# A decoder layer's feed-forward gates on one core: the fourth and fifth products in two levels, and a fixed order of the engines

## The chip, the core and the metric

The kernel runs on one core of one Trainium2 chip. A core has a matrix engine (TensorE, PE in the profile; its weight loads are shown apart as PEld), three engines for element-wise work (VectorE or DVE, ScalarE or ACT, GpSimd or POOL) and SyncE (SP), which here only issues transfers. Matmul results go to eight banks of PSUM, each holding 128 x 512 float32 numbers. The metric is the time of one execution on the device, in microseconds (us).

## The reference

Three blocks, each on a layernorm of x and each added to x: a mamba2 layer followed by an MLP, a product of two fake-quantised matrices, and the feed-forward this case is about (B = 2, S = 512, HID = 1024, INTER = 3584):

```python
def _binary_diff_weight(w, base):
    d = w - base
    coeff = jnp.mean(jnp.abs(d))
    return base + coeff * jnp.sign(d)
W1, W2, W3 = (_binary_diff_weight(w, m) for w, m in ((w1, mean_w1), (w2, mean_w2), (w3, mean_w3)))
gate = jnp.einsum('bsh,ih->bsi', hidden_states, W1)
up = jnp.einsum('bsh,ih->bsi', hidden_states, W3)
h = jax.nn.silu(gate) * up
x = x + jnp.einsum('bsi,hi->bsh', h, W2)
```

## The kernel before

**Stages.** The blocks run one after the other. The MLP of the first block and the feed-forward are both done by `gates` (names with `m` for the MLP and `f` for the feed-forward), which makes the inner values h and writes them to DRAM, and by `down`, which reads them back and multiplies by the last weight. The coefficients and the signs of the feed-forward's weights are made in earlier stages; the signs lie in DRAM as bfloat16.

**Groups and first-level products.** `gates` goes through 14 groups (`NG`, numbered 0 to 13) of 256 inner features. In a group gate and up (128 features by 128 features, two halves) times the activations (1024 features by 2 x 512 tokens) are one 2 x 2 block product, done with Strassen and Winograd's seven products instead of eight. With U2 = product 1 + product 6 and U3 = U2 + product 7, the four blocks are C11 = 1 + 2, C12 = U2 + 5 + 3, C22 = U3 + 5 and C21 = U3 + 4. Each pair of blocks gives gate and up of one quarter, and so a part of h after Silu on ScalarE (L1045) and a product into the tile h on VectorE (L1047).

**Second level.** Each of the seven has an inner size of 512. `second_level` divides two of them at a time by the same rule once more, side by side in the two halves of its banks: 1 with 2 (called the *first* second-level product, banks named `fm`, result in O12) and 6 with 7 (the *second*, banks `fn`, result in O67). There are seven steps, written below as bank and product number; each step is eight instructions of 128 x 256 at L875:

```python
on_pe(lambda: mm("a", 1))
on_act(lambda: nc.scalar.copy(p1, ps["a"]))
on_pe(lambda: mm("b", 6))
on_dve(lambda: add(u2, p1, ps["b"]))
on_pe(lambda: mm("c", 5))
on_pe(lambda: mm("d", 4))
on_pe(lambda: mm("b", 7, True))
on_dve(lambda: add(u3, p1, ps["b"]))
on_dve(lambda: add(c22, u3, ps["c"]))
on_pe(lambda: mm("a", 2, True))
```

A last step, c3, adds onto bank c. So the steps are a1 b6 c5 d4 b7 a2 c3; p1, u2, u3, c22 and c11 are its intermediate sums (`True` means that a step adds onto what the bank holds). Products 5, 4 and 3 are *plain*: `one` (L963) makes each as two columns of 128 x 512 in two banks (`f6c0` and the like, shown as `f6c`, `f6d`), 16 instructions in all. Products 1 and 2 of groups 0 and 1 are made ahead of the stage by `first_two`, in a plain way (L355).

**Sums on VectorE.** `left` makes the weight sums of the next group that products 3, 5, 6 and 7 need, among them the second level's own left sums, and `outer_left` those of the first second-level product. One of `left`'s sums per group, the fourth of one weight (s4), is made later in the MLP's gates (`take_fourths`). `down_blocks` makes four sums (L202, tiles `fw`) of the last weight, which are stored for `down`; `hidden_blocks` makes four sums of h (tiles `fh`). There is one tile h, written to DRAM by SyncE's queue (`fhd`), as are the sums of the last weight (`fwd`).

**Weights.** `ffn_weight` loads the signs on SyncE's queue into a bfloat16 place (`fpl`, two of them, used in turn; L1450), scales them by the coefficient on ScalarE (L1455), and adds the base weight with an accumulating transfer on GpSimd's queue (L1456). Gate and up weights are loaded two groups ahead, the last weight one group ahead, all three issued after the h store of the group before.

**Order.** Two mechanisms exist. `on_pe`, `on_act` and `on_dve` tie an instruction behind the one before it of the same engine (`issue_after`), which makes the order written in the program the order of the engine. What isn't tied is placed by a scheduler, which moves ready work ahead. The MLP's gates (argument `side` set) use the fixed order. In the feed-forward's gates before the change (`side` is None) the lists are empty and so nothing is tied but what stands in `with tc.issue_after(turn)`: the scheduler chooses.

**Down.** `down` makes seven second-level products over all groups (in the order 1, 6, 2, 5, 3, 7, 4; the first also does step e of product 7; L1117) from operand tiles in twelve places (`f1a..`, `f1b..`); its argument `places` says which operand has which place, and `space` leaves room ahead of them, which decides what earlier tiles the places lie over, and so when their loads can start.

## Time and profile before

| | |
|---|---|
| runs, us | 2402.31, 2405.24, 2404.7 (median 2404.7) |
| profiled execution, us | 2406.59 |
| its span, us | 2404.8 |
| granted clock of TensorE, mean | 0.992 |
| feed-forward gates, from and to, us | 1499.5 to 2103.0 |
| busy there: PE, DVE, ACT, POOL, us | 603.5, 421.6, 136.0, 34.3 |
| feed-forward down, from and to, us | 2103.0 to 2404.8 |
| busy there: PE, DVE, ACT, us | 296.7, 167.8, 6.5 |

The span is from the first to the last instruction in the profile of one execution; what the profiled execution takes beside it is 1.8 us. Busy time is the time in which an engine had an instruction, so an engine at full share sets the time of a stage, if its work there is needed. A line of the chain or of the order in time begins with the time from the span's start and the duration, then the engine, the bank or tile and the line of the program, and how many instructions it stands for; what ended an idle time stands in brackets with an arrow. Where two tiles stand with `<-`, the first is written and the others are read.

### The profile page before, as it was taken

What the parts mean: (1) busy time and instruction counts of PE and PEld (TensorE: products, weight loads), DVE (VectorE), ACT (ScalarE), POOL (GpSimd) and SP (SyncE); (2) the same over time, 40 slices, a digit from 0 to 9 for tenths busy, and PEclk for the clock granted to TensorE, in tenths of its full rate; (3) what the DMA queues carried; (4) which work ended last, traced back from release to release, by engine and by line L of the source; (5) the groups of instructions that cost most, each with busy time, mean ns of one, the idle gap of its engine ahead of it and who ended that gap; (6) DMA issues with size and microseconds to landing.
All of it is one profiled execution on the core that took longest, in us unless ns stands there. A gap on an engine that the chain in (4) does not pass through costs nothing.

```text
span 2404.8 us, 23488 instructions
## 1 busy us (share of the span) xinstructions
PE 2356.8 (98%) x8740; PEld 1597.7 (66%) x8740; DVE 1648.5 (69%) x2429; ACT 606.8 (25%) x776; POOL 204.2 (8%) x246
## 2 busy tenths in 40 slices
PE   7999999989999999999999999999999999999999
PEld 5445444446676676677888784676676676688888
DVE  5657777567878878865555656686766766665554
ACT  3345460333243243210000425222222222100000
POOL 1124211201011011000000110000000000000000
PEclk8999999999999999999999999999999999999999
DMA  4353541668888888838746472676676676786651
GB/s 159 114 200 120 186 169 70 176 243 319 306 332 341 303 333 340 289 147 310 222 144 183 130 204 68 182 201 202 163 196 201 166 193 197 243 255 194 192 173 63
DMA packets 183633, 494.49 MB, mean 206 GB/s; under 512 B 21472, under 2 KB 125920, under 8 KB 152544
## 3 DMA queue, kind: packets, MB, share of 16 engines
q1 hardware_dynamic: 155360, 334.65, 40.3%
q0 software_dynamic: 23552, 149.96, 21.7%
q10 hardware_dynamic: 4608, 8.39, 0.9%
q8 instruction: 69, 1.13, 0.2%
q14 instruction: 44, 0.36, 0.0%
HBM read 349.26 MB, written 145.75 MB: 206 GB/s over the span
## 4 chain that ended last, share of the span: by engine, by line
PE 73%; DVE 16%; DMA 4%; issue 3%; ACT 2%; SPq 1%; POOL 0%; DVEq 0%; ACTq 0%; POOLq 0%
PE op L769 3%; DVE sw L202 2%; DVE mpl L199 2%; DVE mo L199 1%; DVE down L202 1%; SPq L1106 1%; DVE mpl L202 1%; ACT smean_w L1273 1%; DVE acc L635 1%; PE ma L355 1%; DMA m4b<-mwd 1%; PE dps L503 1%; PE fa L355 1%; PE xa L1375 1%; DVE mh L1047 1%
## 5 line engine op out<-in xcount | busy, mean ns | idle before, releaser
L1273 ACT ACTIVATE smean_w<-sw 128x2048 bf16<-128x2048 f32 x34 | 65.0, 1911 | 173.5 <-DVE sw L202 173.5
L1455 ACT ACTIVATE fw<-fpl,coeff 128x2048 f32<-128x2048 bf16 x38 | 76.1, 2004 | 91.6 <-DMA fpl<-sign 18.7
L1456 POOL DMA_DIRECT2D fw<-in_mean_w x42 | 36.5, 868 | 530.1 <-ACT fw L1455 476.6
L202 DVE TENSOR_TENSOR sw<-sw,smean_w 128x2048 f32<-128x2048 f32 x34 | 77.6, 2282 | 0.0
L1274 ACT ACTIVATE sw<-sw 128x2048 f32<-128x2048 f32 x34 | 64.9, 1910 | 1.1
L414 POOL TENSOR_TENSOR raw<-raw,base 128x1024 f32<-128x1024 f32 x16 | 41.6, 2602 | 203.6 <-DMA base<-in_mean_w 60.9
L769 PE MATMUL op<-wout,mz 128*128 128x512 f32 x128 | 56.6, 592 | 0.0
L1045 ACT ACTIVATE fo<-fo 128x512 f32<-128x512 f32 x42 | 26.2, 625 | 90.8 <-DVE fo L199 90.7
L1275 POOL DMA_DIRECT2D sign<-smean_w x34 | 18.3, 538 | 292.3 <-ACT smean_w L1273 292.2
L769 PEld LDWEIGHTS op<-wout,mz 128*128 128x128 f32 x128 | 23.9, 190 | 27.7 <-issue 27.3
L202 DVE TENSOR_TENSOR down<-down 128x512 f32<-128x512 f32 x56 | 38.1, 681 | 0.1
L1045 ACT ACTIVATE mo<-mo 128x512 f32<-128x512 f32 x28 | 17.7, 632 | 70.8 <-DVE mo L199 70.8
L199 DVE TENSOR_TENSOR fo<-fo 128x1024 f32<-128x1024 f32 x26 | 31.8, 1225 | 1.7
L355 PE MATMUL fa<-x3T,fw 128*128 128x512 f32 x64 | 30.4, 625 | 2.1 <-ACT fo L361 2.1
L199 DVE TENSOR_TENSOR hid<-hid,op 128x512 f32<-128x512 f32 x24 | 15.9, 683 | 24.0 <-PE op L769 24.0
L1045 ACT ACTIVATE mpl<-mpl 128x512 f32<-128x512 f32 x14 | 8.8, 630 | 89.4 <-DVE mpl L199 89.4
L202 DVE TENSOR_TENSOR fh<-fh 128x512 f32<-128x512 f32 x42 | 29.0, 690 | 1.0
L202 DVE TENSOR_TENSOR mh<-mh 128x512 f32<-128x512 f32 x42 | 28.9, 689 | 0.9
L1264 POOL DMA_DIRECT2D smean_w<-in_mean_w x34 | 18.2, 534 | 129.8 <-DMA sign<-smean_w 42.9
L1375 PE MATMUL xa<-c,c1T 128*128 128x512 bf16 x128 | 28.8, 379 | 0.0
L101 POOL TENSOR_TENSOR q_r<-q_e,mhalf 128x1 f32<-128x1 f32 x8 | 7.0, 877 | 235.2 <-DVE q_e L97 222.1
L1047 DVE TENSOR_TENSOR fh<-fo 128x512 f32<-128x512 f32 x42 | 26.6, 680 | 0.2
(2289 smaller groups left out, 5924.9 us busy)
## 6 DMA issues: line engine op xcount, KB each, us to landing
fw<-in_mean_w POOLq DMA_DIRECT2D x42, 1024.0 KB, 13.6
sw<-in_w POOLq DMA_DIRECT2D x34, 1024.0 KB, 7.7
smean_w<-in_mean_w POOLq DMA_DIRECT2D x34, 1024.0 KB, 7.6
mwd<-down SPq DMA_DIRECT2D x14, 1792.0 KB, 5.7
mhd<-mh SPq DMA_DIRECT2D x13, 1792.0 KB, 10.0
fhd<-fh SPq DMA_DIRECT2D x13, 1792.0 KB, 8.1
fpl<-sign SPq DMA_DIRECT2D x38, 512.0 KB, 8.9
sign<-smean_w POOLq DMA_DIRECT2D x34, 512.0 KB, 6.0
```

Of the source, the lines that this page charges most:

```text
L199: return nc.vector.tensor_tensor(out_, x, y, ALU.add)
L202: return nc.vector.tensor_tensor(out_, x, y, ALU.subtract)
L355: nc.tensor.matmul(ps[x], w[:, 4 * p + k, :P], act[0][:, 4 * p + k, :], start=not p and k == 0, stop=k == 3, skip_group_check=p > 0,)
L414: sub_ = nc.gpsimd.tensor_tensor(w, w, self.base[n % 2], ALU.subtract).ins
L769: nc.tensor.matmul(ps, A[p][:, k, t * P : t * P + P], B[p][:, k, :], start=(k == 0), stop=(k == 3))
L1045: on_act(lambda: nc.scalar.activation(o[:, 0], o[:, 0], AF.Silu))
L1047: nc.vector.tensor_tensor(h[:, slot, :], o[:, 0], o[:, 1], ALU.mult)
L1273: on_act(lambda: nc.scalar.activation(sg, w, AF.Sign))
L1274: on_act(lambda: nc.scalar.activation(w, w, AF.Abs, accum_out=sums[:, j, 2 * i : 2 * i + 1]))
L1375: nc.tensor.matmul(ps, self.c1T[:, k, c : c + P], self.c2[k // 4][:, k % 4, hs], start=(k == 0), stop=(k == KC - 1))
L1455: nc.scalar.activation(dst, src, AF.Identity, scale=coeff[:, j : j + 1])
L1456: nc.gpsimd.dma_start(dst, a[base][i].rearrange("p a b -> p (a b)"), accum_op=ALU.add)
```

## The change

Products 5 and 4 become a third second-level product (banks `fr`, result in O12), from group 2 on, put behind product 3, which now comes first of the plain ones. In groups 0 and 1 products 3, 5 and 4 stay plain and are made in this order, in banks that go round, and `onto` adds them to the blocks. The third product's parts: its left operands come from `third_left` (from the left operands of products 5 and 4), its right ones from `third_right`, once, in group 2, both in VectorE's list between u2 and u3 of the second product. With `early` its step a2 stands ahead of d4: a1 b6 c5 a2 d4 b7 c3. The results are added to C12, C22 and C21 in `finished_third`, run in the next group after its first step, together with the Silus; `last_products` makes the products into h and `put` the sums and the store of h.

`third` being set, the feed-forward's gates use the fixed order of TensorE, ScalarE and VectorE, now for all the sums too (`fix`). Banks go round in eight (X for the first, Y for the second product, Z for product 3 and the third). The sums of the last weight stand behind u2 of the third product (`down_sums`). The two weights of the group after next are asked for at the end of a group and the last weight with the late Silus (`next_weights`). One buffer each instead of two for p1, for the last weight and for each of the two s4 tiles; new tiles for the third's sums (`y54`, `ex`); `down` has no space ahead and other places. Products 1 and 2 of groups 0 and 1 stay as they are. Blank lines are left out below:

```diff
-    def down_blocks(b, t):
+    def down_blocks(b, t, fix=lambda fn: fn()):
...
+        fix(lambda: sub(t3, b22, b12))
...
+    POOLS = dict(t8=1, w=2, w1=2, raw=2, ap=1, hp=1, o1=1, o12=2, o67=1, px=2, s23=1, s4=2, y12=1, y67=1, y54=1, ex=1, b4=2, t4=1)
...
-    def second_level_right(b, t2, t3, t4):
+    def second_level_right(b, t2, t3, t4, fix=lambda fn: fn()):
...
+    def second_level_left(g_, u_, s1, s2, s3, s4, fix=lambda fn: fn()):
...
-    def second_level(name, banks, p1, A, B, O, copied=lambda: None, summed=lambda: None):
+    def second_level(name, banks, p1, A, B, O, copied=lambda: None, summed=lambda: None, early=False):
...
-                        ps[x][:, q, :], A[i][:, q, k, :], B[i][:, q, k, :],
+                        ps[x][:, q, :], A[i][:, q, k, :], B[i][q][:, k, :] if isinstance(B[i], tuple) else B[i][:, q, k, :],
...
         on_pe(lambda: mm("c", 5))
+        if early:
+            on_pe(lambda: mm("a", 2, True))
+            on_act(lambda: nc.scalar.copy(c11, ps["a"]))
         on_pe(lambda: mm("d", 4))
         on_pe(lambda: mm("b", 7, True))
         on_dve(lambda: add(u3, p1, ps["b"]))
         on_dve(lambda: add(c22, u3, ps["c"]))
-        on_pe(lambda: mm("a", 2, True))
-        on_act(lambda: nc.scalar.copy(c11, ps["a"]))
+        if not early:
+            on_pe(lambda: mm("a", 2, True))
+            on_act(lambda: nc.scalar.copy(c11, ps["a"]))
...
-    def gates(name, act, acts, g, pl, weights, down_weight, begun, ex, side):
+    def gates(name, act, acts, g, pl, weights, down_weight, begun, ex, side, third=()):
...
+        fix = on_dve if third else lambda fn: fn()
+        act_last[:] = [None]
+        dve_last[:] = [None]
+        pe_last[:] = [None]
...
+            B12 = B54 = A54 = None
             def outer_left(i, gw, uw):
                 gv, uv = (w[:, :, :P].rearrange("p (q k) c -> p q k c", q=2) for w in (gw, uw))
-                y = pl["y12"].tile([P, 1 if side else 4, 2, 2, P], F32, tag="y", name=f"{name}y12_{i}")
-                if side:
-                    return second_level_left(gv, uv, uv[:, :, :2], y[:, 0], *pl["y12_"])
-                return second_level_left(gv, uv, *(y[:, j] for j in range(4)))
+                more = pl.get("y12_", ())
+                y = pl["y12"].tile([P, 3 - len(more), 2, 2, P], F32, tag="y", name=f"{name}y12_{i}")
+                return second_level_left(gv, uv, uv[:, :, :2], *(y[:, j] for j in range(3 - len(more))), *more, fix=fix)
+            def third_left(i, gw, uw):
+                gv, uv = (w[:, :, P:].rearrange("p (q k) c -> p q k c", q=2) for w in (gw, uw))
+                y = pl["y54"].tile([P, 3, 2, 2, P], F32, tag="y", name=f"{name}y54_{i}")
+                return second_level_left(gv, uv, uv[:, :, :2], *(y[:, j] for j in range(3)), fix=on_dve)
+            def third_right():
+                b5, b4 = (
+                    second_level_right(b.unsqueeze(1), *(x[:, q : q + 1] for x in third), fix=on_dve) for q, b in enumerate((B[5], B[4]))
+                )
+                return {j: (b5[j][:, 0], b4[j][:, 0]) for j in b5}
...
-                    four = pl["s4"].tile([P, 4, P], F32, tag=x, bufs=1 if side and x == "g" else 2, name=f"{name}{x}{i}s4")
-                    sub(two[:, 1], a11, a21)
-                    add(a21, a21, a22)
-                    sub(two[:, 0], a21, a11)
+                    four = pl["s4"].tile([P, 4, P], F32, tag=x, bufs=1 if third or x == "g" else 2, name=f"{name}{x}{i}s4")
+                    fix(lambda: sub(two[:, 1], a11, a21))
+                    fix(lambda: add(a21, a21, a22))
+                    fix(lambda: sub(two[:, 0], a21, a11))
                     fourths.append(lambda four=four, a12=a12, two=two: sub(four, a12, two[:, 0]))
-                    if not side or not i or x == "u":
-                        fourths.pop()()
+                    if not i or x == "u":
+                        fix(fourths.pop())
                     s23.append(two)
                     A.append({3: four, 4: a22, 5: a21})
                 y = pl["y67"].tile([P, 3, 2, 2, P], F32, tag="y", name=f"{name}y67_{i}")
-                return A, second_level_left(s23[0], s23[1], s23[1][:, :, :2], *(y[:, j] for j in range(3)))
+                return A, second_level_left(s23[0], s23[1], s23[1][:, :, :2], *(y[:, j] for j in range(3)), fix=fix)
...
+                more = third and i > 1
+                if more:
+                    X, Y, Z = ([(4 + 14 * (i - 2) + o + j) % 8 for j in range(6)] for o in (0, 4, 8))
+                    X, Y = X[:4], Y[:4]
                 def one(x, p, onto=False, into={}):
                     if not onto:
-                        into[x] = [bank(X["ccdd".index(x) + j], f"{name}{i}{x}{j}") for j in range(2)]
+                        into[x] = [bank((Z if more else X)["ccdd".index(x) + j], f"{name}{i}{x}{p}{j}") for j in range(2)]
...
                 if i in begun:
                     O12 = begun[i]
+                    for part in late:
+                        part()
+                    take_fourths()
...
-                    c, d = one("c", 5), one("d", 4)
+                    c, d = (one("c", 3), one("d", 5)) if third else (one("c", 5), one("d", 4))
                 p1 = pl["px"].tile([P, 2, Q], F32, tag="p", name=f"{name}p67_{i}")
                 O67 = pl["o67"].tile([P, 2, 2, L], F32, tag="o", name=f"{name}o67_{i}")
                 def summed67(i=i, O12=O12):
-                    if side:
-                        side(on_dve)
+                    nonlocal A54, B54
+                    side(on_dve)
+                    if i > 1:
+                        on_dve(lambda: add(O12[:, 1], O12[:, 0], O12[:, 1]))
+                    if third:
+                        if i == 2:
+                            B54 = third_right()
                         if i > 1:
-                            on_dve(lambda: add(O12[:, 1], O12[:, 0], O12[:, 1]))
+                            A54 = third_left(i, *coming[0])
+                        on_act(lambda: nc.scalar.activation(O12[:, 1, 0], O12[:, 1, 0], AF.Silu))
                 second_level(f"{name}n{i}", Y, p1, A67, B67, O67, summed=summed67)
                 on_dve(lambda: add(O67[:, 0], O12[:, 0], O67[:, 0]))
                 turn = on_dve(lambda: add(O67[:, 1], O67[:, 0], O67[:, 1]))
-                if i:
-                    c = one("c", 5)
-                for j in range(2):
-                    add(O12[:, 0, j], O67[:, 1, j], c[j])
-                if i:
-                    d = one("d", 4)
-                for j in range(2):
-                    blocks21 = add(O67[:, 1, j], O67[:, 1, j], d[j]).ins
-                one("c", 3, True)
+                h = pl["hp"].tile([P, 7, L], F32, tag="h", name=f"{name}h{i}")
+                if third:
+                    turn = on_dve(lambda: nc.vector.tensor_tensor(h[:, 0, :], O12[:, 1, 0], O12[:, 1, 1], ALU.mult))
+                def onto(o, u, v, fix=lambda fn: fn().ins):
+                    for j in range(2):
+                        ins = fix(lambda: add(o[:, j], u[:, j], v[j]))
+                    return ins
+                C12, C22, C21 = O67[:, 0], O12[:, 0], O67[:, 1]
+                if more:
+                    c = one("c", 3)
+                elif third:
+                    if i:
+                        c, d = one("c", 3), one("d", 5)
+                    onto(C12, C12, c)
+                    onto(C12, C12, d)
+                    onto(C22, C21, d)
+                    onto(C21, C21, one("c", 4))
+                else:
+                    if i:
+                        c = one("c", 5)
+                    onto(C22, C21, c)
+                    if i:
+                        d = one("d", 4)
+                    blocks21 = onto(C21, C21, d)
...
                     with tc.issue_after(turn):
-                        outer = i > 0 and i + 1 not in begun
-                        if outer and not side:
+                        A, A67 = left(i + 1, *coming[0])
+                        if i > 0:
                             A12 = outer_left(i + 1, *coming[0])
-                        A, A67 = left(i + 1, *coming[0])
-                        if outer and side:
-                            A12 = outer_left(i + 1, *coming[0])
...
+                def down_sums(i=i, last=last):
+                    b, sums_to, store = w2.pop(0)
+                    with tc.issue_after(begin if last else turn):
+                        down_blocks(b, sums_to(), fix)
+                    store(dram[1][i])
+                def next_weights(i=i, last=last):
+                    if not last:
+                        w2.append(down_weight(i + 1, stored))
+                if not third and i + 2 < NG:
                     coming.append(weights(i + 2, stored))
-                if not side and not last:
+                if more:
+                    onto(C12, C12, c, on_dve)
+                    p1 = pl["px"].tile([P, 2, Q], F32, tag="p", name=f"{name}p54_{i}")
+                    second_level(f"{name}r{i}", Z[2:], p1, A54, B54, O12, summed=down_sums, early=True)
+                else:
+                    down_sums()
+                if third and i + 2 < NG:
+                    coming.append(weights(i + 2, stored))
...
+                def finished_third(parts=parts, more=more, C12=C12, C22=C22, C21=C21, O12=O12, next_weights=next_weights):
+                    if more:
+                        on_dve(lambda: add(C12, C12, O12[:, 0]))
+                        on_dve(lambda: add(C22, C22, C21))
+                        on_dve(lambda: add(C21, C21, O12[:, 1]))
+                    for o, _ in parts:
+                        on_act(lambda: nc.scalar.activation(o[:, 0], o[:, 0], AF.Silu))
+                    next_weights()
+                def last_products(parts=parts, h=h):
+                    for o, slot in parts:
+                        on_dve(lambda: nc.vector.tensor_tensor(h[:, slot, :], o[:, 0], o[:, 1], ALU.mult))
...
+                if third:
+                    late.extend([finished_third, last_products, put])
...
+                if last:
+                    for part in late:
+                        part()
...
-    pl = open_pools(g, "f", ("o12", "o67", "px", "s23", "s4", "y12", "y67", "ap", "w", "w1"))
+    pl = open_pools(g, "f", ("o12", "o67", "px", "s23", "s4", "y12", "y67", "ap", "w", "w1"), dict(px=1))
...
-            nc.scalar.activation(dst, src, AF.Identity, scale=coeff[:, j : j + 1])
+            on_act(lambda: nc.scalar.activation(dst, src, AF.Identity, scale=coeff[:, j : j + 1]))
...
-    pl.update(open_pools(g, "f", ("hp", "b4", "t4")))
+    pl.update(open_pools(g, "f", ("hp", "b4", "t4", "y54", "ex"), dict(b4=1)))
...
+    more = pl["ex"].tile([P, 3, D], F32, tag="ex", name="fex")
+    third = [more[:, k].rearrange("p (q b c) -> p q b c", q=2, b=2) for k in range(3)]
...
-    dram = gates("f", x3T, acts, g, pl, ffn_weights, ffn_down, {0: begun0, 1: begun1}, ex, None)
+    dram = gates("f", x3T, acts, g, pl, ffn_weights, ffn_down, {0: begun0, 1: begun1}, ex, lambda dve: None, third)
     reloaded("f", xd)
-    down("f", dram, 14336, (9, 10, 11, 4, 2, 3, 5, 8, 0, 1, 6, 7), store, lambda: None)
+    down("f", dram, 0, (9, 4, 5, 6, 2, 3, 11, 10, 7, 8, 0, 1), store, lambda: None)
```

## The prediction

> **What bounds the kernel now.** I read the page's busy shares first, then busy time by stretch for the second feed-forward (its gates run from 1499.5 to 2103.0 us), then the chain of waits and the order in time over one group there. The page first, then two stretches (columns: length, then busy us and count of PE, PEld, DVE, ACT, POOL, granted clock, DMA share, GB/s):
>
> ```profile
> PE 2356.8 (98%) x8740; PEld 1597.7 (66%) x8740; DVE 1648.5 (69%) x2429; ACT 606.8 (25%) x776; POOL 204.2 (8%) x246
> ```
> ```profile
> 1609.55:2058.13 448.58, 448.58 (x1601) 302.35 (x1600) 311.11 (x467) 102.22 (x108) 24.86 (x29) 1.00 0.68 192
> 1462.84:1467.50 4.66, 4.66 (x7) 2.02 (x8) 1.88 (x5) 3.94 (x6) 1.08 (x2) 0.63 0.01 2
> ```
>
> The first stretch is ten groups: TensorE is never idle, 44.86 us a group, and VectorE works 31.1 us of each. So the group is bound by matmul time alone. The chain of waits of group 6 prices the parts:
>
> ```profile
> 1751.19 1.73 PE fm6b L875 x8
> 1752.92 1.73 PE fm6a L875 x8
> 1754.65 1.77 PE fm6c L875 x8
> ...
> 1768.54 6.87 PE f6c L963 x16
> 1775.41 6.87 PE f6d L963 x16
> 1782.28 6.87 PE f6c L963 x16
> ```
>
> A step of a second-level product is 1.73 us, seven are 12.1 (12.13 with the small wait inside); a plain product is 6.87. 2 x 12.13 + 3 x 6.87 = 44.87. The next view is VectorE's order in time:
>
> ```profile
> 1724.52 1.23 DVE L199 TENSOR_TENSOR fo<-fo,fo 128x1024 f32<-128x1024 f32 x1
> 1725.77 1.22 DVE L199 TENSOR_TENSOR fo<-fo 128x1024 f32<-128x1024 f32 x1
> 1726.92 0.68 DVE L202 TENSOR_TENSOR fy<-fw,fw 128x512 f32<-128x512 f32 x1
> 1727.52 0.68 DVE L199 TENSOR_TENSOR fo<-fo,f5c 128x512 f32<-128x512 f32 x1
> ...
> 1745.84 0.69 DVE L202 TENSOR_TENSOR fh<-fh 128x512 f32<-128x512 f32 x1
> 1746.57 0.69 DVE L199 TENSOR_TENSOR fh<-fh 128x512 f32<-128x512 f32 x1
> ...
> 1752.96 0.69 DVE L199 TENSOR_TENSOR fo<-fp,fm6b 128x512 f32<-128x512 f32 x1 [3.77 <-PE fm6b L875]
> 1753.68 0.69 DVE L199 TENSOR_TENSOR fo<-fo,fm6c 128x512 f32<-128x512 f32 x1
> ```
>
> Starts count, not durations: a 512-wide sum follows an independent one after 0.60 us, one that it needs after 0.72; a 1024-wide one holds VectorE 1.15, or 1.25 before a dependent one. A sum on a bank starts 0.20 us after the step before it ends (1752.76 to 1752.96).
>
> **The saving.** From group 2 on, products 5 and 4 (13.74 us) become one second-level product of 12.09: 1.65 us less TensorE time, 12 times, 19.8 us. All else below is against it.
>
> **The third product's own wait.** Its order is a1 b6 c5 a2 d4 b7 c3. c3 adds onto bank c, which c22 must have read, and c22 follows u3, which needs b7. In the old order a2 stands between b7 and c3: u3 at 1752.96, c22 at 1753.68, done 1754.37, and c3 starts when a2 ends, 1.73 after b7. Now nothing stands there, so 0.20 + 0.72 + 0.69 + about 0.13 = 1.73 us is idle. That alone takes back the 1.65.
>
> **VectorE is later than that.** A group gets 49 operations of 512 and six of 1024 (before: 44 and three; five new combining sums of the third product, four `third_left`, three 1024 ones that add it in, four plain bank sums fewer), in one fixed order. From the end of the second product (t = 0): its last u2 at 0.20, two 1024 sums at 1.00 and 2.25, the product into h at 3.40, then the 15 sums of `left` and `outer_left` from 4.00. Before, the scheduler mixed these with others and each took 0.60; now 11 of 15 follow the one they need: 11 x 0.725 + 4 x 0.60 = 10.38, so the two sums of product 3 start at 14.38 and u2 of the third product at 15.58, done 16.27. TensorE: product 3 until 6.87, a1 to d4 until 15.51; b7 overwrites what u2 reads and starts at 16.40 (0.89 idle), ends 18.13. VectorE has the four down-weight sums at 16.18, 16.78, 17.50, 18.23, u3 at 18.83, c22 at 19.55, done 20.24; c3 runs 20.37 to 22.10 (2.24 idle). The group is 24.27 + 22.10 = 46.37, or 1.51 more than 44.86. The tail (u2, three 1024 sums) takes VectorE until 4.7 us into the next group, whose first bank isn't needed before 6.9: no more is lost there. Groups 2 to 12 have these sums: 11 x 1.51 = **16.6**. Group 13 has no `left`: +0.1.
>
> **Groups 0 to 2.** Before, TensorE filled group 0's waits with products of group 1:
>
> ```profile
> 1522.82 1.93 PE L875 MATMUL fn0c<-ft,fy 128*128 128x256 f32 x8
> 1524.59 5.50 PE L963 MATMUL f1d<-ft,fw 128*128 128x512 f32 x12
> 1529.92 3.60 PE L963 MATMUL f0c<-x3T,fg0s 128*128 128x512 f32 x8
> ```
>
> The fixed order forbids that. Product 4 of group 0 takes product 3's bank, free after u2, two 1024 sums, the h product and one sum: 0.20 + 0.80 + 1.25 + 1.15 + 0.60 + 0.68 + 0.13 = 4.8 us idle. Then, on the same clock (0 is the end of group 0's second product), TensorE is through product 4 at 11.7; VectorE's order brings the sum that frees the next bank at 11.7, and the `left` sum that b6 of group 1's second product multiplies at 15.5, where TensorE could start b6 at 13.5: 0.15 + 2.1 idle. b7 could start at 20.8, but u2 stands behind four down-weight sums, three products into h, four h sums and the late s4 and is done at 24.65: 4.0 idle. 0.8 goes to the stage's first bank, which ScalarE is still copying. Group 1 itself has product 5 between, so no wait: **11.9** to the start of group 2. In group 2 the eight `third_right` and four `third_left` sums stand between u2 and u3 of the second product: 15.78 + 0.60 + 1.15 + 5.55 + 2.78 puts u3 at 25.9 rather than 20.97: **4.9**.
>
> **Weights and queues.** Old, three accumulating loads went out together and landed after 8.9, 13.4 and 16.2 us. Now the down weight goes alone, after the late Silus, about 7.5 us into a group; I take 9 us. SyncE's queue then has its store and behind it that of h (8.1 to landing): 25. The next write of h, at 27.7, waits for that store since there is one buffer. 2.7 us of cover; if it goes, all of VectorE's list is late. One buffer for p1 and b4: the copy waits for u3, done a step earlier; the b4 store has landed a group earlier. Both nothing. The two ScalarE scalings (2.0 each) start when a2 and d4 of the third product end and are done before the next p1 copy; with two more copies (0.6 each) ScalarE still works 12 us of a group: nothing. On GpSimd's queue only the order of issue in time changes; each waits for its own scaling.
>
> **Into the down stage.** Before, product 3 covered the last sums. Now they follow c3: VectorE has eight until `f1b12` can be made (52.05 + 2.02 from group 13's start), product 7 starts at 54.2 instead of 51.6: **+2.6**. The stores of h stay under products 1, 7 and 2. The other tile places only decide when loads can start: a11 earlier, a21 and b12 during product 3. Nothing.
>
> Sum: 16.6 + 0.1 + 11.9 + 4.9 + 2.6 = 36.1, 2440.9.
>
> **The clock.** These waits are long enough to ask if TensorE slows. The rows:
>
> ```profile
> 1462.84 1.41 PE L355 MATMUL fa<-x3T,fw 128*128 128x512 f32 x2 [2.08 <-ACT fo L361]
> 1164.76 1.53 PE L1117 MATMUL mo6b<-mw6e,mh6e 128*128 128x256 f32 x6 [2.27 <-DVE mw6e L199]
> ```
>
> After 2.08 idle the seven instructions of the 1462.84 stretch took 4.66 us at a clock of 0.63, where 7 x 0.43 is 3.0: 1.65 lost. After 2.27 us none was. The Trainium skill (TensorE: Matmul & The Clock Gate, part 1) says that the clock halves after an idle window of some 3.4 us, windows run free, and gaps up to about 3 us are safe. By it only the two long waits (4.0 and 4.9) cost, 3.3: 2444. By the row, gaps of 2.24 cost in about half the groups, by where the window falls: 5.5 x 1.65 = 9.1, and the 3.2-us wait before product 7 1.7 more: 2455. I take the row.
>
> **Rivals.** *VectorE in time*: chains run at 0.60 here, the third product loses its own 1.73 and no more: 2404.8 + 1.2 + 11.9 + 4.9 + 2.6 + 3.3 = 2429. For it: VectorE would still be idle 3 us a group; against: the 0.72 rows. *Faster*: c3 never waits, because bank c's readers are done when b7 ends; 19.8 less, and TensorE's order at the start costs the rest of it back only in part (+5): 2390. It decides if c22 is done by 17.2 us after the second product; the rows have 20.2. *The h store late*: if the down weight takes 16.2 to land, as the third did, the store lands at 32 and VectorE waits 4.5 in each of 11 groups: 2505. *No effect*: saving and wait cancel (1.65 against 1.73) and the start hides: 2405.
>
> **The numbers.** Forecast, with the clock effect from none to all, 0.66; in time 0.12; h store 0.13; faster 0.06; no effect 0.03. Spread of the forecast: no clock loss 2441, all gaps 2466. The range reaches to VectorE in time below and part of the store's wait above: 2428 to 2482. 0.2% (4.8 us) is what a measurement here tells from no change. The sum is against the span of 2404.8; its execution took 2406.6 and the runs' median is 2404.7, so it stands for the median as it is: 2455. Faster 0.06, same 0.03, slower 0.91.
>
> **What would show it.** Groups of 46 to 48 us; idle before TensorE's `fr` c3 of about 2.2 and before b7 of 0.9, both ended by VectorE; 11 to 12 us lost before `fm2`, 5 in `fn2`; clock rows under 1 in some groups. Wrong if c3 waits under 1 us, or if VectorE's h product waits for a DMA.

## The result and the profile after

The changed kernel takes 2459.9 us (median; 2454.6 to 2464.8), the kernel before 2403.5 (2397.7 to 2405.2): 2.4% slower, ratio 1.0239 with a 95% interval of 1.0208 to 1.0269. The forecast was 2455, range 2428 to 2482. The profiled execution has a span of 2461.2 us. Two single runs of kernels further down, 4155 us of start_free and 14076 us of filled, lie far outside the scatter of their kernels and are left out of the medians there.

Busy shares of the whole span, and busy time over groups 3 to 12 (columns as in the prediction's stretches):

```profile
PE 2365.0 (96%) x9020; PEld 1666.7 (68%) x9028; DVE 1755.4 (71%) x2537; ACT 618.4 (25%) x800; POOL 204.6 (8%) x246
```
```profile
1630.42:2108.42 478.00, 450.95 (x1842) 355.69 (x1840) 394.76 (x550) 112.02 (x128) 24.31 (x28) 0.97 0.64 177
```

TensorE, never idle in these ten groups before, is idle for 27.0 us of them, and its clock is 0.97. A group takes 47.8 us in place of 44.86, and VectorE works 39.5 us of it instead of 31.1. Where a group waits is seen in TensorE's order in time, here in group 3 (a line's last bracket is the idle time ahead of it and what ended it):

```profile
1668.45 1.89 PE L875 MATMUL fr3d<-fex,fw 128*128 128x256 f32 x8
1671.08 1.99 PE L875 MATMUL fr3b<-fex,fy 128*128 128x256 f32 x8 [0.73 <-DVE fo L199]
1675.05 1.13 PE L875 MATMUL fr3c<-x3T,fy 128*128 128x256 f32 x4 [1.98 <-DVE fo L199]
1676.02 1.55 PE L875 MATMUL fr3c<-ft,fy 128*128 128x256 f32 x4
1677.36 3.10 PE L875 MATMUL fm4a<-x3T,fw 128*128 128x256 f32 x8
```

Starts count here too: a step should follow after 1.727, so b7 (1668.45 to 1671.08) is 0.90 late and c3 (1671.08 to 1675.05) 2.24. The last line has eight instructions in 3.10 us; in the kernel before the same eight took 1.89, and the difference is the clock. VectorE's order in group 6, with the second product's end at 1799.10 (its sum on the bank starts 0.20 later):

```profile
1799.30 0.69 DVE L199 TENSOR_TENSOR fo<-fo,fn6c 128x512 f32<-128x512 f32 x1 [1.37 <-PE fn6c L875]
1800.10 1.23 DVE L199 TENSOR_TENSOR fo<-fo,fo 128x1024 f32<-128x1024 f32 x1
1801.36 1.23 DVE L199 TENSOR_TENSOR fo<-fo 128x1024 f32<-128x1024 f32 x1
1802.50 0.68 DVE L1044 TENSOR_TENSOR fh<-fo 128x512 f32<-128x512 f32 x1
1803.10 0.68 DVE L202 TENSOR_TENSOR fg7s<-fw 128x512 f32<-128x512 f32 x1
...
1814.75 0.68 DVE L199 TENSOR_TENSOR fo<-fp,fr6b 128x512 f32<-128x512 f32 x1
1815.35 1.28 DVE L202 TENSOR_TENSOR fw6t<-fw 128x512 f32<-128x512 f32 x2
1816.67 1.42 DVE L202 TENSOR_TENSOR fw6t<-fw,fw6t 128x512 f32<-128x512 f32 x2
1818.01 0.68 DVE L199 TENSOR_TENSOR fo<-fp,fr6b 128x512 f32<-128x512 f32 x1
1818.72 0.69 DVE L199 TENSOR_TENSOR fo<-fo,fr6c 128x512 f32<-128x512 f32 x1
```

So u2 of the third product starts 15.65, u3 18.91 and c22 19.62 us after the second product's end, with no idle time between. The clock is seen in the stretches around c3 of group 3, one at full clock and the next at half:

```profile
1672.97:1676.38 3.41, 1.43 (x7) 1.20 (x7) 2.66 (x4) 0.11 (x1) 0.86 (x1) 1.00 1.04 210
1676.38:1679.80 3.42, 3.42 (x10) 2.71 (x9) 2.06 (x3) 0.00 (x0) 0.00 (x0) 0.50 0.98 235
```

From c3 to the next group's c3 it is 46.46 us where the clock stays full (1628.59 to 1675.05) and 48.13 where it doesn't (1771.33 to 1819.46): a stretch of half clock costs 1.7 us. Eight of the groups 3 to 12 have one; from the gates' start to the start of the down stage's product 6 there are twelve.

To place the difference, three stretches that meet, measured between first instructions of products: *start*, from the first of the products that are made ahead for groups 0 and 1 (L355) to group 3; *groups*, from group 3 to group 13; *end*, from group 13 to the down stage's product 6. Everything behind them takes 258.6 us in both kernels, and what lies ahead differs by 1.3.

| us | start | groups | end |
|---|---|---|---|
| before | 159.3 | 448.6 | 88.1 |
| after | 181.5 | 478.0 | 94.2 |
| difference | +22.2 | +29.4 | +6.1 |
| of it half clock | 3 x 1.7 | 8 x 1.7 | 1 x 1.7 |
| predicted without the clock | +18.3 | +15.1 | +2.7 |

### The profile page after: what moved, and what is told of

Same layout as the page of the kernel before. It is cut to its first block, busy times and chain, and to the rows that moved or that the text cites. A ratio compares the mean times of both kernels' runs of the same rounds, so it can differ in the third digit from the quotient of the medians.

```text
span 2461.2 us, 24247 instructions
## 1 busy us (share of the span) xinstructions
PE 2365.0 (96%) x9020; PEld 1666.7 (68%) x9028; DVE 1755.4 (71%) x2537; ACT 618.4 (25%) x800; POOL 204.6 (8%) x246
## 4 chain that ended last, share of the span: by engine, by line
PE 63%; DVE 26%; issue 4%; DMA 3%; ACT 2%; SPq 1%; POOL 1%; DVEq 0%; POOLq 0%; ACTq 0%
PE op L769 3%; DVE fo L199 3%; DVE sw L202 2%; DVE mpl L199 2%; DVE fy L202 2%; SPq L1179 1%; DVE mo L199 1%; DVE down L202 1%; DVE fw L199 1%; DVE mpl L202 1%; ACT smean_w L1346 1%; DVE acc L635 1%; PE dps L503 1%; PE ma L355 1%; PE fa L355 1%
## 5 line engine op out<-in xcount | busy, mean ns | idle before, releaser
L199 DVE TENSOR_TENSOR fo<-fo,fo 128x1024 f32<-128x1024 f32 x50 | 61.2, 1225 | 3.5
L414 POOL TENSOR_TENSOR raw<-raw,base 128x1024 f32<-128x1024 f32 x16 | 43.2, 2698 | 201.8 <-DMA base<-in_mean_w 59.1
L1348 POOL DMA_DIRECT2D sign<-smean_w x34 | 18.3, 539 | 291.2 <-ACT smean_w L1346 291.1
L199 DVE TENSOR_TENSOR fw<-fw 128x512 f32<-128x512 f32 x52 | 35.9, 691 | 1.7
L202 DVE TENSOR_TENSOR fy<-fw,fw 128x512 f32<-128x512 f32 x48 | 33.0, 688 | 0.8
L355 PE MATMUL fa<-x3T,fw 128*128 128x512 f32 x64 | 29.2, 605 | 2.5 <-ACT fo L361 2.5
L1123 ACT ACTIVATE fo<-fo 128x512 f32<-128x512 f32 x42 | 25.6, 628 | 18.3 <-DVE fo L199 18.1
## 6 DMA issues: line engine op xcount, KB each, us to landing
mhd<-mh SPq DMA_DIRECT2D x13, 1792.0 KB, 10.6
```

The lines of the kernel that those rows point to most:

```text
L199: return nc.vector.tensor_tensor(out_, x, y, ALU.add)
L202: return nc.vector.tensor_tensor(out_, x, y, ALU.subtract)
L355: nc.tensor.matmul(ps[x], w[:, 4 * p + k, :P], act[0][:, 4 * p + k, :], start=not p and k == 0, stop=k == 3, skip_group_check=p > 0,)
L414: sub_ = nc.gpsimd.tensor_tensor(w, w, self.base[n % 2], ALU.subtract).ins
L1123: on_act(lambda: nc.scalar.activation(o[:, 0], o[:, 0], AF.Silu))
```

## The experiments

All times are medians, beside the kernel before in the same session (2401 to 2404). The stretches are those of one profiled execution. What lies ahead of them is the same program in every kernel, yet took from 1442 to 1454 us, so a small difference is read from the stretches and not from the medians.

| | us | ratio, 95% interval | start | groups | end |
|---|---|---|---|---|---|
| order_only | 2424.5 | 1.0090 (1.0062 to 1.0118) | 169.8 | 448.6 | 98.0 |
| dve_moved | 2433.1 | 1.0126 (1.0092 to 1.0160) | 178.9 | 449.8 | 93.7 |
| a2_late | 2497.0 | 1.0389 (1.0360 to 1.0418) | 183.0 | 508.5 | 92.9 |
| both | 2475.6 | 1.0295 (1.0262 to 1.0328) | 179.5 | 488.9 | 95.5 |
| store_apart | 2481.9 | 1.0334 (1.0312 to 1.0357) | 184.1 | 490.4 | 94.2 |
| start_free | 2457.5 | 1.0222 (1.0190 to 1.0253) | 174.5 | 477.8 | 93.5 |
| right_early | 2457.8 | 1.0225 (1.0199 to 1.0252) | 180.1 | 478.0 | 93.2 |
| filled | 2431.3 | 1.0117 (1.0096 to 1.0139) | 175.8 | 447.6 | 97.3 |
| filled_u2 | 2420.7 | 1.0069 (1.0044 to 1.0095) | 176.0 | 438.7 | 98.2 |
| places_old | 2463.2 | 1.0250 (1.0226 to 1.0274) | 183.1 | 478.2 | 93.5 |
| best | 2417.1 | 1.0055 (1.0036 to 1.0074) | 168.1 | 441.8 | 101.5 |
| best_2 | 2409.5 | 1.0033 (1.0017 to 1.0049) | 161.0 | 439.4 | 102.3 |

**The fixed order alone.**

```diff
-    dram = gates("f", ..., ex, lambda dve: None, third)
+    dram = gates("f", ..., ex, lambda dve: None)
```

> The third product is left out: products 5, 4 and 3 stay plain and the feed-forward's gates run in the fixed order that the MLP's gates have; the other places stay. My theory (the loss comes from the third product's own waits, from VectorE's list behind it and from the first groups): a group takes 45.2 us as the MLP's groups do in the profile before, 0.36 more than 44.86, some 4 us over all groups, and 2 to 6 us at the start: 2405 to 2416, about 2410. Rival (a fixed order in itself costs a group its time, whatever the products): groups of 46 us and more, 2430 or above.

2424.5, above my range and under the rival's. Its ten groups take 448.58 us, to the hundredth what they took before (I had expected 45.2 a group): the order costs a group nothing. The start is 10.4 us longer and the end 10.0, so 20 us are lost at the two borders without any third product, to the order or to the single buffers and places that this kernel keeps from the change. (For the start best_2, below, points to the order; for the end no run separates these.) The longest waits of TensorE there are 4.6 us before group 0's last plain product, as long as in the changed kernel though the plain products stand in the old order, and 8.9 us before the down stage's product 7, ahead of which VectorE waits 5.6 us for a load of h. What the groups lose is the third product's.

**Which wait is whose.** Two edits, alone and together.

```diff
-    second_level(f"{name}r{i}", ..., summed=down_sums, early=True)
+    second_level(f"{name}r{i}", ..., summed=down_sums)                 (a2_late)
+    second_level(f"{name}r{i}", ..., summed=outer_sums, then=down_sums, early=True)   (dve_moved)
```

`outer_sums` is `outer_left`, taken out of the sums after the second product; `then` is called behind c22.

> VectorE's list alone: the four sums for the next group's first product stand behind u2 of the third product, the four of the down weight behind its c22. My theory: u2 is done before d4 ends, so no wait before b7, and before c3 the 1.73 us that its chain takes by itself: groups of 44.95 at full clock, 11 x 1.5 = 16 us less, 2444; 2430 if a single wait of 1.7 us leaves the clock alone. Rival (VectorE's list is the bound): 2455 to 2460.

2433.1, near the 2430 that I gave for the case that the single wait leaves the clock alone. The chain of waits in group 6 of this kernel:

```profile
1801.94 1.73 PE fr6d L875 x8
1803.67 1.74 PE fr6b L875 x8
1805.41 0.02 issue
1805.43 0.70 DVE fo L199
1806.13 0.02 issue
1806.16 0.70 DVE fo L199
1806.85 0.04 issue
1806.90 1.13 PE fr6c L875 x4
```

b7 follows d4 at once; c3 waits for u3 and c22 and for nothing else. Groups are 44.98 us (expected 44.95), and none has a half-clock stretch, though each has an idle time of 1.5. This is the world of the prediction's rival *VectorE in time* (2429). So the loss in the groups is these two waits and the clock that they cost, and the order of VectorE's list makes 1.5 us of the 3.1 as well as all of the clock.

> The third product's step a2 goes back between b7 and c3. My theory: the wait before c3 falls from 2.25 to 0.5 us of TensorE, the one before b7 stays at 1.0, a group takes 44.7 us where the clock is full: 11 x 1.73 = 19 us less, and up to 13.5 less if these shorter waits no longer cost the clock: 2427 to 2441. Rival (VectorE's list is the bound, so TensorE waits for it wherever its steps stand): the wait only moves, 2455 to 2460.

2497.0: worse, against my theory, and by more than the rival allowed. Two things were wrong in it. b7 waits for u2 on VectorE; with a2 taken from ahead of b7, TensorE comes to b7 1.73 earlier and waits that much longer, so the idle time only moves, as the rival said. And there is a new wait. ScalarE and VectorE in group 6 of this kernel:

```profile
1835.75 0.59 ACT L897 COPY fo<-fr6a 128x512 f32<-128x512 f32 x1 [16.19 <-PE fr6a L875]
1836.23 3.90 ACT L1528 ACTIVATE fw<-fpl,coeff 128x2048 f32<-128x2048 bf16 x2
```
```profile
1817.04 0.69 DVE L1044 TENSOR_TENSOR fh<-fo 128x512 f32<-128x512 f32 x1 [3.42 <-DMA fhd<-fh]
```

The two scalings of the next weights stand on ScalarE behind the copy of a2 (shown at the end of group 6; the wait shown follows from those at the end of group 5, at 1784.9). Their accumulating loads are now issued 6.3 and 4.4 us before that of the down weight (14.5 and 12.6 in the changed kernel). The down weight's store, and behind it that of h, go out 22.0 us after the start of the group (1807.9 and 1785.9) rather than 16.4, and VectorE's product into the only h tile waits for the store: 33.9 us in 12 groups, where the changed kernel has 8.2 in two (groups 1 and 13). This is the prediction's rival with the late store of h, at its place and about its price (4.5 foreseen, 3.4 in group 6). In groups 2 to 12 of the changed kernel it did not happen, and the place of a2 is the only difference.

> Both of these edits. My theory: no wait in groups 3 to 12, 43.2 us each, no clock loss there; start and end as they are: 11 x 3.24 = 36 us less for the waits and 13.5 less for the clock, 2410 (2405 to 2416). Rival (with the third product VectorE has more to do than fits): groups of 44.9 us or more with waits for VectorE, 2430 or above.

2475.6, in the rival's range, but for the reason just seen: the same wait for the store, 45.4 us in 12 groups, hides what the edits save.

```diff
-    stored = nc.sync.dma_start(dram[0][i], h).ins
+    stored = (nc.gpsimd if third else nc.sync).dma_start(dram[0][i], h).ins
```

> The kernel with the late a2 (2497), but the store of h goes out on GpSimd's queue, so that it no longer stands behind the down weight's store on SyncE's. My new theory (with a2 late both scalings start 22 us later, so the three accumulating loads run together, the down weight lands late, the store of h waits behind its store, and VectorE's product into h, with all behind it, for that): VectorE no longer waits for the store, a group takes 44.7 us at full clock, 2427 to 2441. Rival (the loads themselves are late for the sums on VectorE, or the transfers are short of bandwidth): VectorE waits for another transfer instead, 2480 or more.

2481.9. The queue is a part of it: in group 6 VectorE waits 0.90 for the store and no longer 3.42. But the groups don't fall to 44.7, since my number forgot what a2_late had just shown: b7 waits 0.9 + 1.73 + 0.9 = 3.5 (3.45 in group 6), and with that idle time the clock is halved in each of groups 3 to 12. Neither theory's number holds; the rival's range does, for another reason than it gave.

**The first groups.**

```diff
-        act_last[:] = [None]
-        dve_last[:] = [None]
-        pe_last[:] = [None]
+        for x in (act_last, dve_last, pe_last):
+            x[:] = [] if third else [None]
...
+                if third and i == 2:
+                    for x in (act_last, dve_last, pe_last):
+                        x[:] = [None]
```

> The changed kernel with groups 0 and 1 untied: the fixed order begins with group 2. My theory: the two long waits of 4.5 and 3.9 us before group 2 go as TensorE takes up other products meanwhile, with them one or two half-clock windows of 1.7: 8 to 12 us less, 2448 to 2452. Rival (the waits lie in the new order of the products 3, 5, 4 and their shared banks, not in the tying): 2457 to 2462.

The median (2457.5, three runs from 2447.7 to 2460.6) doesn't move beyond its scatter. The three stretches together are 8.0 us shorter, 7.1 of it in the start (what lies ahead of them took 5.0 longer in this execution), so the tying made some of the start's waits, as order_only also says; but untied work meets the one h tile. TensorE and VectorE in group 1:

```profile
1565.74 9.60 PE L989 MATMUL f1c<-ft,fw 128*128 128x512 f32 x16 [5.98 <-DVE fo L199]
```
```profile
1557.92 0.69 DVE L1046 TENSOR_TENSOR fh<-fo 128x512 f32<-128x512 f32 x1 [7.08 <-DMA fhd<-fh]
```

VectorE stands 7.1 us at the product into h, now made before the last bank's sums, and product 4, which needs product 3's bank again, stands 6.0 with it, at half clock afterwards. Both causes are there: the tying, and the order of the products with their shared bank.

```diff
                     end()
+                    if third and i == 2:
+                        B54 = third_right()
...
-                        if i == 2:
-                            B54 = third_right()
```

> The changed kernel with the eight sums of the third product's right operands ahead of the second product's u2 in group 2, behind the first product's sums, rather than between u2 and u3. My theory: VectorE has 3.7 us idle there that they fill, so the wait of 4.9 before c3 of group 2's second product falls to some 1.2, and its half-clock window goes: 4 to 5.5 us less, 2455; in the profile group 2 starts its third product that much sooner. Rival (VectorE has no such gap in group 2): the wait moves to b7 of the second product, 2460.

2457.8, between the two forecasts, so the profile must decide: the start is 1.5 us shorter, which is one half-clock stretch less. The waits moved (2.8 of idle time before b7 and 1.5 before c3 of the second product, for 4.7 before c3): the rival is right, VectorE had no gap for these eight sums there.

**Filling c3's wait.**

```diff
+        fill()
         on_pe(lambda: mm("c", 3, True))
...
+                def next_step(i=i, last=last):
+                    nonlocal done
+                    if not last:
+                        done = first_step(f"{name}m{i + 1}", (4 + 14 * (i - 1)) % 8, A12, B12)
...
-                    second_level(f"{name}m{i}", X, p1, A12, B12, O12, first, summed)
+                    second_level(f"{name}m{i}", X, p1, A12, B12, O12, first, then=summed, done=done)
```

The edit stands on dve_moved's list of VectorE. `first_step` makes a1 of the next group's first product; `fill` calls it between b7 and c3; `then=summed` puts the three late products into h behind the first product's c22.

> VectorE's list as in the kernel that took 2433, and besides the first step (a1) of the next group's first product between b7 and c3 of the third, and the three late products into h behind that first product's c22. My theory: what is left of the loss in a group is the 1.73 us that c3 must wait for its chain; other work of TensorE can fill it: groups of 43.2 to 43.6 us, 11 x 1.4 = 15 to 17 us less, 2417. Rival (VectorE is then the bound, or the store of h comes late as with the late a2): groups stay at 45 us or more, 2433 or above.

2431.3, just under the rival's range. Groups take 44.73; c3 no longer waits, but b7 of the next first product does, 1.3 us, for its u2, which stood behind the three sums of 1024 that add the third product in. That is a matter of VectorE's order, which neither side had named, and the next edit tests it: u2 goes ahead of these sums.

```diff
-    second_level(f"{name}m{i}", X, p1, A12, B12, O12, first, then=summed, done=done)
+    second_level(f"{name}m{i}", X, p1, A12, B12, O12, summed=first, then=summed, done=done)
```

> The filled kernel (2432), with u2 of the next group's first product ahead of the three sums that add the third product in, rather than behind them. In the filled kernel TensorE's wait had moved to that product's b7, 1.3 us, for u2. My theory: VectorE has room for both once the order is right: no wait in a group, 43.3 to 43.6 us, 11 x 1.2 = 13 us less, 2418. Rival (VectorE's 40 us of work and the store of h leave no room, so each wait taken away comes back at another step): 2428 or above.

2420.7, 2.7 over the expectation. Groups take 43.87 on average (43.3 to 44.3), 0.99 less than before the change, and TensorE is idle in the ten of them for 2.7 us in place of 27.0. What remains are short waits of TensorE for VectorE, which itself waits for the store of h (22.8 us in 12 groups). The start and the end still cost 17 and 10 us.

**Other places.** The twelve places of the down stage as before the change:

```diff
-    down("f", dram, 0, (9, 4, 5, 6, 2, 3, 11, 10, 7, 8, 0, 1), store, lambda: None)
+    down("f", dram, 0, (9, 10, 11, 4, 2, 3, 5, 8, 0, 1, 6, 7), store, lambda: None)
```

> The changed kernel with the twelve operand places of the down stage as before the change (no space ahead of them still). My theory (the places only decide when loads can start, which TensorE's work covers): 2455 to 2464, as the changed kernel. Rival (the other places pay for part of the late down start, or cause it): 3 us or more away from it, with the start of the down stage's sixth product that much moved.

2463.2, and the end takes 93.5 us against 94.2: the places by themselves are not the cause of the late down stage. The space ahead of them was not put back alone.

**Towards a faster version.** Beside the edits of filled_u2, groups 0 and 1 as before the change (untied, products 5, 4, 3), the right operands' sums at the end of group 1, and group 13 untied and plain (parts of the edit are left out, here and below).

```diff
+        tie(not third)
...
+                more = third and 1 < i < NG - 1
+                if third and i in (2, NG - 1):
+                    tie(i == 2)
+                if third and last:
+                    for b in (B[5], B[4]):
+                        add(b[:, :2, Q:], b[:, :2, Q:], b[:, :2, :Q])
...
+                if third and i == 1:
+                    B54 = third_right()
```

> Besides this, groups 0 and 1 untied and with products 5, 4, 3 in the old order, the right operands' sums at the end of group 1 where the scheduler may place them, and group 13 untied with plain products (the right operands of products 5 and 4 put back by two sums). My theory: start and end as before, give or take 4 us for the eight sums; groups 2 to 12 at 43.4 us, 11 x 1.45 = 16 us less than before: 2388 to 2394. Rival (the fixed order of groups 2 to 12 costs its waits again at each border to the untied groups, or the groups keep 44.9): 2403 or above.

2417.1: in the rival's range. The ten groups are faster than before by 6.8 us, but the start and the end lose 8.8 and 13.4. ScalarE at the start of this kernel:

```profile
1522.99 2.00 ACT L1564 ACTIVATE fw<-fpl,coeff 128x2048 f32<-128x2048 bf16 x1 [13.65 <-DMA fpl<-sign]
1524.89 0.57 ACT L901 COPY fo<-fn0a 128x512 f32<-128x512 f32 x1
```

The copy that group 0's sums need was ready to go at 1516 and stands behind a scaling that waits for its signs; TensorE stood 6.6 us. At the other end, the first load of `f1b` in group 13 lay over a tile that the group's second product reads; SyncE's queue stood 4.9 us for it, with all loads behind, and TensorE stood 8.6 before the down stage's product 7. Whether these two waits are the whole loss is what the next edit asks.

```diff
         tie(not third)
+        act_last[:] = [None]
...
-    down("f", dram, 0, (9, 4, 5, 6, 2, 3, 11, 10, 7, 8, 0, 1), store, lambda: None)
+    down("f", dram, 14336, (1, 10, 8, 2, 11, 9, 3, 0, 4, 5, 6, 7), store, lambda: None)
```

> The kernel called best (2417), with two edits. Its profile showed groups 2 to 12 faster than before, and 15 us lost before group 2 and 13 us from group 13 to the down stage: at the start the copy of a second-level result on ScalarE stood behind a scaling that waited 13.7 us for its signs (there is one buffer for the last weight now), and at the end SyncE's queue held all down loads behind one whose place lay over a tile in use until group 13's second product. So ScalarE is tied from the start, and the down operands get the space and places that are free when group 13 begins. My theory: 10 to 12 us come back at each end, with the half-clock windows there: 2393 to 2400, below the kernel before. Rival (VectorE's 40 us a group are the cause at the borders, not these two waits): 2410 or above.

2409.5, just under the rival's range and 0.33% above the kernel before (interval 0.17% to 0.49%): no version beat it. The start came back (161.0) with the single buffers kept, and from its first product to product 6 the down stage is as fast as before (42.5 against 43.2), but group 13 ahead of it takes 59.8 us in place of 44.9, so the end is as long as it was. VectorE in group 13 of this kernel:

```profile
2063.00 0.68 DVE L202 TENSOR_TENSOR fw13t<-fw 128x512 f32<-128x512 f32 x1
2074.28 2.03 DVE L202 TENSOR_TENSOR f1a<-f1a,f1a 128x1792 f32<-128x1792 f32 x1 [10.60 <-DMA fhd<-fh]
...
2077.55 0.68 DVE L199 TENSOR_TENSOR fo<-fp,fn13b 128x512 f32<-128x512 f32 x1
```

With the loads out early the scheduler put the first sum of the down stage ahead of u3 of group 13's second product, the load behind it was late, and VectorE stood 10.6 us; c3 of that product waited 10.3, and ran its first 3.4 us at half clock. That this sum alone is what the version lacks was not tried.

## Why the prediction was right

**The third product's wait and VectorE's lateness** held to a tenth: u2 at 15.65 (foreseen 15.58), u3 at 18.91 (18.83), c22 at 19.62 (19.55), b7 late by 0.90 (0.89), c3 by 2.24 (2.24), a group at full clock 46.46 (46.37). `dve_moved` shows the split: 1.73 is the chain's own, the rest VectorE's list. *VectorE in time* fell with it; *faster* too, since c22 is done at 20.3, 3.1 us after the point from which that rival decides.

**The first groups.** From start to start, the waits were 4.7, 3.9 and 4.9 (4.8, 4.0 and 4.9 foreseen); that of 2.1 before b6 of group 1 was 0.6, the one wait that was read wrong. With group 2's share it is +18.3 foreseen, and 22.2 less 5.1 for the clock, 17.1, measured.

**The weights' order.** In groups 2 to 12 VectorE never waits for the store of h, as foreseen. It does in groups 1 and 13, 4.1 us each, which the prediction had named as a sign of being wrong; no wait of TensorE follows from either: in group 1 it works from 1553.2 to 1577.4 and beyond without a gap, and in group 13 VectorE is idle again before u2. That the cover is thin, and that a2's place holds it, was shown by a2_late. One buffer for the last weight was costed at nothing; nothing in the changed kernel speaks against it, but in `best` the scaling that waited for its signs was of that weight.

**Into the down stage** the term was mis-sized: 6.1 less one half-clock stretch is 4.4, not 2.7. VectorE in group 13 of the changed kernel shows what was left out:

```profile
2140.24 0.69 DVE L1044 TENSOR_TENSOR fh<-fo 128x512 f32<-128x512 f32 x1 [4.09 <-DMA fhd<-fh]
...
2143.25 0.69 DVE L199 TENSOR_TENSOR fo<-fp,fr13b 128x512 f32<-128x512 f32 x1 [1.13 <-issue]
...
2148.43 2.02 DVE L202 TENSOR_TENSOR f1a<-f1a,f1a 128x1792 f32<-128x1792 f32 x1 [3.29 <-DMA f1b<-fwd]
...
2151.70 0.68 DVE L199 TENSOR_TENSOR fo<-fp,fr13b 128x512 f32<-128x512 f32 x1
...
2162.29 2.02 DVE L202 TENSOR_TENSOR f1b<-f1b,f1b 128x1792 f32<-128x1792 f32 x1 [0.16 <-DMA f1a<-fhd]
```

The delay by the store of h (first line) has been made up at u2 (second line), ahead of which VectorE is idle again. Then a sum of the down stage, with its wait of 3.29 for a load, stands ahead of u3: b7 ends at 2149.90, so u3 could have started at 2150.10 and is 1.6 late, an estimate from the pace of 0.20 behind a step. What follows is late by as much: the sum of `f1b` that product 7 needs starts 53.9 us after the group, where 52.05 was foreseen. That is about the 1.7 that the term lacked.

**The clock** was mis-sized too: 14 us foreseen by the row, twelve stretches of 1.7, 20.4, measured. The mechanism, that it depends on where a window falls, was right. In these traces every half-clock stretch lasts 3.41 us or a multiple of it, and their starts lie whole multiples of 3.41 apart (1676.38, 1724.17 and 1771.96, for instance, fourteen each), so the time is cut into fixed windows. Group 7 of the changed kernel, which kept its clock, and the prediction's row of 2.08 us, which didn't, cut in this way:

```profile
1864.12:1867.53 3.41, 1.49 (x7) 0.96 (x6) 3.31 (x6) 1.51 (x1) 1.72 (x2) 1.00 0.79 192
1867.53:1870.94 3.41, 3.35 (x16) 2.96 (x17) 1.90 (x4) 0.00 (x0) 0.00 (x0) 1.00 0.90 163
```
```profile
1460.15:1463.56 3.41, 1.33 (x4) 0.48 (x3) 2.90 (x5) 3.41 (x7) 0.00 (x0) 1.00 0.19 77
1463.56:1466.97 3.41, 3.41 (x5) 1.35 (x5) 1.16 (x5) 3.22 (x5) 1.08 (x2) 0.50 0.01 2
```

TensorE is idle for 1.92 us of the first window and full clock follows; it is idle for 2.08 of the third line's (in group 3, above, for 1.98), and half clock follows. Over all fourteen traces, in the windows at full clock from 1499 to 2170 us, half clock followed 107 of 108 windows with 1.97 us of idle time or more, and none of the 2518 with less (in earlier stages, with other matmuls, the border lay between 1.74 and 1.99). The prediction's other row, 2.27 us that cost nothing, was cut by a border into 0.70 and 1.58. The wait of 0.7 us before b7 plays no part: where half clock follows, it lies in the window before, and groups 7 and 12 had it too; there the longer wait was cut by a border.

Eight groups of ten pay, and not the half that was foreseen, because a paid stretch makes the next group's wait fall well again: the group takes 48.13 us, 14.1 windows, so the wait moves by 0.3 us along its window and stays whole for four groups (3 to 6, 8 to 11). The fifth is cut, takes 46.46 us, 13.6 windows, and the next four are whole. A wait at a random place would be whole in 0.42 of the groups (1.43 of 3.41 us), an estimate from these figures.

By the rule that was weighed, of the Trainium skill (TensorE: Matmul & The Clock Gate, part 1 and "Why this matters for your kernels": half clock after an idle window of about 3.4 us, no gaps above some 3 us), only the long waits at the start and the one before the down stage would have paid. The free-running window is what these traces show. The limit is lower here: 2 us of idle time within one window is enough.

All terms together: 37 us without the clock (36.1 foreseen) and 20 for the clock (14). That the first sum comes so close is in part luck: the start was 1.2 too high, the groups 0.7 and the end 1.7 too low.

## What to carry to other kernels

A product that saves TensorE time and adds sums can lose all of it in front of its last dependent step (dve_moved), and pays in its group when that step finds other work in front of it (filled_u2): cost the chain from the bank to the next step in starts, then look for a step of the next product to put there. In a fixed order, a step that only moves takes its waiters along; name the engine that the *next* step waits for before counting a gain, and look at the queues that a copy holds back (a2 carried two loads and, through them, the store of h). At the borders of a fixed order, check what a scheduler put there: in best_2 a sum of the next stage ahead of the last chain held VectorE for 10.6 us. To price the clock, lay TensorE's idle time over the fixed windows and not gap by gap.

## What was not expected of the hardware

What halves TensorE's clock here is neither the length of a gap nor two gaps close together, but the idle time inside one of the fixed windows of 3.41 us: in the stages of this case half clock for the whole of the next window after 1.98 us of it or more, full clock after 1.96 or less. The same wait of 1.98 us therefore cost 1.7 us in eight of groups 3 to 12 and nothing in two, and the single 1.5 of dve_moved nothing in any group.
